# Sums of exponentials in four column tiles with a repeating load of the inverses, and convolutions in column halves beside layer 1

## The chip, the cores and the metric

The kernel runs on one core of a Trainium2 chip, in fp32 throughout. The metric is the device time of one execution in microseconds (us), from the median of several runs; lower is better. The engines of the core run side by side, each through its own queue in order: TensorE (PE, with its weight loads shown as PEld), VectorE (DVE), ScalarE (ACT), GpSimd (POOL), and SyncE (SP), which here only issues DMAs.

## The reference

The input x has 4 images of 128 channels and 64 x 64 positions, so S = 4096 positions per image. Two layers follow one another; the second ends with a mixture of experts.

```python
# layer 0: x + attention over positions, from 1x1 convolutions
xn    = group_norm(x)                       # 32 groups
e1    = prelu(w1 @ xn)                      # 64 channels (queries)
e2    = prelu(w2 @ xn)                      # 64 channels (keys)
asm   = prelu(wa @ xn)                      # 128 channels (values)
score = softmax(e1.T @ e2, axis=keys)       # 4096 x 4096 per image
x     = x + score @ asm.T
# layer 1: tokens t = x.T (4096 x 128)
t = t + softmax(q @ k.T / 128) @ v          # q, k, v from layer_norm(t)
t = t + expert_ffn(layer_norm(t))           # 64 experts, top 8 tokens of each
```

The softmax of layer 0 needs, for each query position, the sum of exponentials over all 4096 keys, and the product with the values is divided by it.

## The kernel before

**Tiling.** An image is cut into 8 blocks of 512 positions (`NB = 8`, `BLK = 512`). For a block of queries the keys are walked through in 8 steps (`NG = 8`) of 512 keys each. In a step, TensorE makes the scores of the current step (`ps`, L526), ScalarE takes their exponentials (`pt`, L535), and TensorE makes the products of the exponentials of the step before with the values (`av`, L460 in layer 0, L488 in layer 1). In layer 0 both matmul groups use TensorE as two row tiles (64 rows by 128 columns, printed as 64\*128). In layer 1 both use it as two column tiles (128\*64): the tuple `SCORE_COLS[1]` holds the two column halves. Everything that is fp32 goes through TensorE in two passes, so a matmul shows as two instructions.

**Stages and order.** `stage(b, layer, beside, then)` runs the attention of one image and layer as 64 steps. The order is written by hand: stages go (0,0), (1,0), (0,1), (2,0), (1,1), (3,0), (2,1), (3,1) as (image, layer). At each step, `step_after()` advances the finishing work of an earlier block by one segment, the query of the next block is prepared, and the generator `beside` advances by one segment. A `yield` in such a generator ends its segment. `tc.no_sync_barrier()` closes the step, so that instructions keep to their steps.

**Convolutions.** `conv(b)` computes e1, e2 and asm of an image, block by block, three segments each: normalise a block (`xn`); one matmul for e1 and e2 together (`pe`, L264, 128 by 128 weights, 512 columns moved); four matmuls for asm (`pa`, L280, 128 columns moved each). They run on the full array (128\*128). `conv(0)` and `conv(1)` run in the layer-0 stage (0,0); `conv(2)` runs beside the layer-1 stage (0,1) and `conv(3)` beside the layer-1 stage (1,1).

**Finishing a block of layer 0.** DVE adds the exponentials of all steps into `sacc` (L550), so that each of the 128 partitions holds the sum over its share of the keys. `finish_conv` then has three segments:

1. ScalarE copies the two halves of the product out of PSUM (`u`, `c0`), POOL adds them, DVE folds `sacc` to 128 x 512 (`c1`), POOL adds `c1` to a guard tile `all_sum`.
2. A matmul with a 128 x 128 matrix of ones (`pd`, L572) adds `c1` over the partitions and leaves each sum on all 128 partitions; DVE takes the reciprocal (`inv`, L574); POOL multiplies `u` by it (L575), adds it into a guard tile `all_inv` (L576) and adds the residual (`xp`, L578).
3. DVE transposes `xp` in 32 x 32 blocks (`xt`, L306) and SP stores it to DRAM for layer 1 (`xT`, L313).

`finish_conv` runs once per block: 32 times, 29 of them in steps of a layer-0 stage and 3 (block 7 of images 1, 2 and 3) in the first steps of a layer-1 stage. `finish_attn` does the same for layer 1, in eight segments; its matmuls `pv` (L614) and `pg` (L663), and the query matmul `pq` (L429), are in column halves already.

**Buffers.** `ms_tile` gives one of two PSUM banks to all small matmuls (`pd`, `pe`, `pa`, `pv`, `pg`, `pq`). `block_tile("inv", ...)` has two buffers in SBUF. POOL's queue carries `u`, `all_sum`, `all_inv`, `xp`, and the powers of -0.5 that layer norm needs (`l_y`, L174).

Of the kernel before, what the change touches and what calls it, by code (L numbers as in the profile page):

```python
# [15 lines left out]
P = 128  # L16
BLK = 512
# [5 lines left out]
SCORE_COLS = {0: (slice(0, P),), 1: (slice(0, P // 2), slice(P // 2, P))}  # L23
# [3 lines left out]
def tile_unshifted(  # L27
# [14 lines left out]
    nc = tc.nc  # L42
    x = a["x"]
    B, C, S = x.shape
# [4 lines left out]
    NB = S // BLK  # L49
    NJ = S // P  # L50
    SUB = BLK // P
# [24 lines left out]
    def ms_tile(name):  # L76
        return ps_ms.tile([P, BLK], F32, tag="ms", name=name)

    def block_tile(tag, name, bufs=2):
        pool = pools[of_pool.get(tag, "blk")]  # L80
        return pool.tile([P, BLK], F32, tag=tag, name=name, bufs=bufs)

    def dram_tile(shape, name):
        return dram.tile(shape, F32, tag=name, name=name)
# [6 lines left out]
    t2 = [[dram_tile([P, BLK], f"t2_{b}_{n}") for n in range(NB)] for b in range(B)]  # L91
    x1T = [[dram_tile([P, SUB, C], f"xT_{b}_{n}") for n in range(NB)] for b in range(B)]
    tokens = [dram_tile([S, C], f"tk_{b}") for b in range(B)]
    first_pair = dram_tile([P, S], "first_pair")

    e1 = [[dram_tile([CR, BLK], f"e1_{b}_{n}") for n in range(NB)] for b in range(B)]

    def load_block(tag, src, name, bufs):
        t = block_tile(tag, name, bufs)
        nc.sync.dma_start(out=t, in_=src)  # L100
        return t
# [6 lines left out]
    for i, q in enumerate((nc.sync, nc.scalar, nc.sync, nc.scalar)):  # L108
        part = bass.ts(i, S // 4)
# [8 lines left out]
    w12 = const_load("w12", [P, 2 * CR], a["w12T"])  # L118
    b12 = const_load("b12", [P, 1], a["b12"])
    a12 = const.tile([P, 1], F32, tag="a12", name="a12")  # L120
    for i, al in enumerate(("a1", "a2")):
        nc.scalar.dma_start(
            out=a12[i * CR : (i + 1) * CR, :], in_=a[al].partition_broadcast(CR)
        )
    wa = const_load("wa_sb", [P, C], a["waT"])
# [8 lines left out]
    for h in range(2):  # L134
# [6 lines left out]
    ones = const.tile([P, P], F32, tag="ones", name="ones")  # L141
# [8 lines left out]
        out=last, in_=last, compare_op=ALU.is_ge, fill=0.0, base=1 - P, pattern=[[0, P]],  # L150
# [9 lines left out]
        out=avg_g3, in_=avg_g3, compare_op=ALU.is_ge, fill=0.0, base=0,  # L160
# [3 lines left out]
        out=avg_g3, in_=avg_g3, compare_op=ALU.is_ge, fill=0.0, base=GS - 1,  # L164
# [18 lines left out]
    def group_norm(b, first=None):  # L183
        st = small.tile([P, NB, 6], F32, tag="gn_st", name=f"gn_st{b}")

        def pair(i):
            if i == NB // 2:
                return []
            if first is not None:
                return [first[:, bass.ts(2 * i + h, BLK)] for h in range(2)]  # L190
            return [
                load_block("xs", x_of(b, 2 * i + h), f"g{b}_{2 * i + h}", 4) for h in range(2)
            ]

        coming = pair(0)
        yield
        for i in range(NB // 2):
            blocks, coming = coming, pair(i + 1)
            for h in range(2):
                nc.vector.bn_stats(out=st[:, 2 * i + h, :], in_=blocks[h])  # L200
            yield
        mv = small.tile([P, 2], F32, tag="gn_mv", name=f"gn_mv{b}")
        nc.vector.bn_aggr(out=mv, in_=st.rearrange("p n s -> p (n s)"))
        yield
        pm = ms_tile(f"gn_pm{b}")
        nc.tensor.matmul(pm[:, 0:1], lhsT=avg_g, rhs=mv[:, 0:1], start=True, stop=True)
        ab = const.tile([P, 2], F32, tag=f"gn{b}", name=f"gn{b}")
        nc.vector.tensor_copy(ab[:, 0:1], pm[:, 0:1])
        d = small.tile([P, 2], F32, tag="gn_d", name=f"gn_d{b}")
        nc.vector.tensor_sub(d[:, 0:1], mv[:, 0:1], ab[:, 0:1])  # L210
        nc.vector.scalar_tensor_tensor(
            d[:, 1:2], in0=d[:, 0:1], scalar=d[:, 0:1], in1=mv[:, 1:2], op0=ALU.mult, op1=ALU.add
        )
        yield
        pv = ms_tile(f"gn_pv{b}")
        nc.tensor.matmul(pv[:, 0:1], lhsT=avg_g, rhs=d[:, 1:2], start=True, stop=True)
        inv_sqrt(ab[:, 1:2], pv[:, 0:1], GN_EPS, 1, f"gn{b}")
        gn[b] = ab
        yield
# [22 lines left out]
        for h in range(2):  # L242
            nc.sync.dma_start(out=q[h * CR : (h + 1) * CR, :], in_=src)

    def conv(b, whole=None):


        kA = seq.tile([P, NP, P], F32, tag="k", name=f"e2_{b}")
        vT = seq.tile([P, NJ, C], F32, tag="v", name=f"asm{b}")
        keys[b, 0], values[b, 0] = kA, vT  # L250

        def block(n):
            if whole is None:
                return load_block("xs", x_of(b, n), f"ck{b}_{n}", 4)
            return whole[:, bass.ts(n, BLK)]

        xb = block(0)
        for n in range(NB):
            xn = normed(b, xb, f"xk{b}_{n}")
            if n + 1 < NB:  # L260
                xb = block(n + 1)
            yield
            pe = ms_tile(f"pe{b}_{n}")
            nc.tensor.matmul(pe, lhsT=w12, rhs=xn, start=True, stop=True)  # L264
            y, t = block_tile("ye", f"ye{b}_{n}"), block_tile("te", f"te{b}_{n}")
            nc.scalar.activation(y, pe, AF.Identity, bias=b12)
            prelu([(y, lambda z: z)], y, t, a12)
            y4 = y[CR:, :].rearrange("c (p h t) -> c p h t", h=2, t=P)
            for h in range(2):
                nc.sync.dma_start(  # L270
                    out=kA[h * CR : (h + 1) * CR, bass.ts(n, SUB // 2), :], in_=y4[:, :, h, :]
                )
            if whole is not None and n == 0:
                spread_query(b, n, y[:CR, :])
            else:
                nc.sync.dma_start(out=e1[b][n], in_=y[:CR, :])
            yield
            pa = ms_tile(f"pa{b}_{n}")
            for s in range(SUB):
                nc.tensor.matmul(  # L280
                    pa[:, bass.ts(s, P)], lhsT=xn[:, bass.ts(s, P)], rhs=wa, start=True, stop=True
                )
            y2, t2 = block_tile("ye", f"ya{b}_{n}"), block_tile("te", f"ta{b}_{n}")
            y3 = y2.rearrange("p (s c) -> p s c", c=C)
            nc.vector.tensor_tensor(
                y3, pa.rearrange("p (s c) -> p s c", c=C),
                ba.unsqueeze(1).to_broadcast([P, SUB, C]), op=ALU.add,
            )
            prelu(
                [(vT[:, bass.ts(n, SUB), :], lambda z: z.rearrange("p (s c) -> p s c", c=C))],  # L290
                y2, t2, aa,
            )
            yield
# [9 lines left out]
    SQ = 32  # L303
# [256 lines left out]
    def finish_conv(b, n):  # L560
        nm = f"{b}_0_{n}"
        av = avs.pop((b, 0, n))
        u, c0, c1 = (block_tile(t, f"{t}{nm}") for t in ("u", "c0", "c1"))
        s2 = sums.pop((b, n))
        nc.scalar.copy(u, av[:, 0, :])
        nc.scalar.copy(c0, av[:, 1, :])
        nc.gpsimd.tensor_add(u, u, c0)
        nc.vector.tensor_add(c1, s2[:, 0, :], s2[:, 1, :])  # L568
        nc.gpsimd.tensor_add(all_sum, all_sum, c1)  # L569
        yield  # L570
        pd = ms_tile(f"pd{nm}")
        nc.tensor.matmul(pd, lhsT=ones, rhs=c1, start=True, stop=True)  # L572
        r = block_tile("inv", f"inv{nm}")
        nc.vector.reciprocal(r, pd)  # L574
        nc.gpsimd.tensor_mul(u, u, r)  # L575
        nc.gpsimd.tensor_add(all_inv, all_inv, r)  # L576
        xp = block_tile("xp", f"xp{nm}")
        nc.gpsimd.tensor_add(xp, resid.pop((b, 0, n)), u)  # L578
        yield
        turn_to_tokens(xp, block_tile("tb", f"xt{nm}"), x1T[b][n])  # L580
# [200 lines left out]
    def chain(*gens):  # L781
        for g in gens:
            yield from g
# [4 lines left out]
    def stage(b, layer, beside, then, ahead=None, pace=(6, 3)):  # L788

        coming = iter(())
        for k in range(pace[0]):
            next(ahead or iter(()), None)
        for n, g in attention(b, layer):
            step_after()
            if g == 1:
                coming = query(b, layer, n + 1) if n + 1 < NB else then and query(*then, 0)
                coming = coming or iter(())
            next(coming, None)  # L800
            if n == 0 and ahead:
                for _ in range(pace[1]):
                    next(ahead, None)
            else:
                next(beside, None)
            tc.no_sync_barrier()
        run(coming)
        run(beside)
# [38 lines left out]

    stage(0, 0, chain(group_norm(1), conv(1), weights_qk()), (1, 0), ahead=first_conv, pace=(3, 3))
    stage(1, 0, chain(group_norm(2), attn_keys(0), mix_values(0)), (0, 1))
    stage(0, 1, chain(group_norm(3), conv(2)), (2, 0))  # L850
    stage(2, 0, chain(done_after(route(0, take_from_seq(0))), attn_keys(1), mix_values(1)), (1, 1))
    stage(1, 1, conv(3), (3, 0))
    stage(3, 0, chain(done_after(route(1, take_from_seq(1))), attn_keys(2), mix_values(2)), (2, 1))
    stage(2, 1, attn_keys(3), (3, 1))
    ends["prep"].close()
# [118 lines left out]
    for i in range(B // 2):  # L974
        pe = ms_tile(f"poe{i}")
# [6 lines left out]
        for n in range(NB):  # L982
            px = sc_tile(f"px{i}_{n}")
            for h in range(2):
# [3 lines left out]
                    start=True, stop=True,  # L988
# [541 lines left out]
```

## Time and profile before

| | |
|---|---|
| median of 3 runs | 3368.74 us (3368.69 to 3370.04) |
| profiled execution | 3368.98 us |
| its span, first to last instruction | 3367.3 us |
| TensorE clock granted, mean | 0.986 |
| TensorE busy | 3261.8 us, 97% of the span |
| DVE, ACT, POOL busy | 2179.4, 1244.3, 432.2 us |
| `pd` matmuls (L572) | 64 instructions, 36.0 us |
| `pe` and `pa` matmuls (L264, L280) | 64 and 256 instructions, 37.6 and 38.2 us |
| reciprocal of layer 0 (L574) | 32 instructions, 3356 ns each |

Busy time counts a stretch once per group of instructions, so that groups whose instructions overlap add up to more than the engine's own busy time. Starts in the timeline are therefore a better measure of what a matmul costs than its listed duration: TensorE starts the next group before the last one has drained. The rows of the timeline are printed as start in us, length in us, engine, line, operation, output<-inputs, the tile of the array that is used, shape, and count of instructions in the row.

### The profile page before, as it was taken

Reading aid. Unit: us, or ns where it says so; the run is one execution under the profiler, and the core shown is the slowest. Engines: PE = TensorE matmul, PEld = TensorE weight load, DVE = VectorE, ACT = ScalarE, POOL = GpSimd, SP = SyncE. Lnnn points to the kernel's source line nnn. Section 1 sums busy time; section 2 is a strip of 40 time slices with the busy share of each in tenths; the row PEclk is TensorE's granted clock in tenths of the full one; section 3 lists DMA queues with packets and bytes.
Section 4 is the critical chain, followed back from the end, with each engine's and each line's share of the span. In section 5 each row is a group of like instructions: output and inputs, shape, how many; then the busy total and the mean of one; then the engine's idle time right before and its main releaser. Section 6 shows DMA issues by size and latency. Waiting matters only on the chain. (4 is left out here: it accounts for less than half of the span.)

```text
span 3367.3 us, 48432 instructions
## 1 busy us (share of the span) xinstructions
PE 3261.8 (97%) x19392; PEld 1539.9 (46%) x19392; DVE 2179.4 (65%) x4184; ACT 1244.3 (37%) x1417; POOL 432.2 (13%) x409
## 2 busy tenths in 40 slices
PE   7999999999999999999999999999999999999955
PEld 4444444444444444444445444444454545445432
DVE  6665577556675667756766567865775656765654
ACT  2333333333333344333333334333333333433320
POOL 0111122310000013230000003251000001100000
PEclk9999999999999999999999999999999999999977
DMA  3121122011110112201210111310321101120169
GB/s 86 44 47 24 37 55 62 19 32 40 40 41 23 36 26 51 62 16 29 47 36 19 30 33 54 69 39 18 66 47 27 26 23 32 32 70 16 26 239 348
DMA packets 359354, 174.13 MB, mean 52 GB/s; under 512 B 275280, under 2 KB 300752, under 8 KB 358864
## 3 DMA queue, kind: packets, MB, share of 16 engines
q1 hardware_dynamic: 351408, 159.71, 18.5%
q10 hardware_dynamic: 7200, 10.20, 0.8%
q8 instruction: 154, 2.52, 0.3%
q0 software_dynamic: 512, 1.05, 0.1%
q14 instruction: 80, 0.66, 0.1%
HBM read 110.20 MB, written 56.23 MB: 49 GB/s over the span
## 5 line engine op out<-in xcount | busy, mean ns | idle before, releaser
L535 ACT ACTIVATE pt<-ps 128x1024 f32<-128x1024 f32 x1024 | 1020.8, 1024 | 1566.3 <-PE ps L526 1475.3
L526 PE MATMUL ps<-q,t 128*64 128x512 f32 x4096 | 927.4, 594 | 0.0
L460 PE MATMUL av<-pt,asm 64*128 64x512 f32 x4096 | 922.1, 589 | 0.9 <-ACT sw L597 0.9
L550 DVE TENSOR_TENSOR sacc<-sacc,pt 128x1024 f32<-128x1024 f32 x448 | 570.5, 1273 | 203.3 <-ACT pt L535 171.9
L488 PE MATMUL av<-pt,tt 128*64 128x256 f32 x3072 | 638.0, 380 | 0.0
L460 PEld LDWEIGHTS av<-pt,asm 64*128 64x128 f32 x4096 | 396.1, 187 | 485.0 <-issue 470.5
L474 DVE TENSOR_TENSOR tt<-pt 128x512 f32<-128x512 f32 x512 | 353.4, 690 | 371.0 <-ACT pt L535 352.3
L488 PE MATMUL av<-tt,mixed 128*64 128x256 f32 x2048 | 527.4, 380 | 5.2 <-DVE tt L474 5.2
L526 PEld LDWEIGHTS ps<-q,t 128*64 128x64 f32 x4096 | 290.6, 137 | 497.8 <-issue 462.8
L526 PE MATMUL ps<-e,e 64*128 64x512 f32 x2048 | 490.5, 597 | 2.4 <-ACT pt L535 2.4
L488 PEld LDWEIGHTS av<-pt,tt 128*64 128x64 f32 x3072 | 354.1, 137 | 291.4 <-issue 143.2
L488 PE MATMUL av<-pt,mixed 128*64 128x256 f32 x1024 | 305.5, 380 | 0.0
L488 PE MATMUL av<-tt,tt 128*64 128x256 f32 x1024 | 305.5, 380 | 0.0
L526 PEld LDWEIGHTS ps<-e,e 64*128 64x128 f32 x2048 | 192.3, 187 | 245.9 <-issue 238.2
L488 PEld LDWEIGHTS av<-tt,mixed 128*64 128x64 f32 x2048 | 281.1, 137 | 8.8 <-DVE tt L474 6.1
L174 POOL TENSOR_TENSOR l_y<-l_v,mhalf 128x4 f32<-128x4 f32 x64 | 64.7, 1011 | 1691.3 <-DVE l_v L173 1691.3
L476 DVE TENSOR_TENSOR tt<-pt 128x256 f32<-128x256 f32 x512 | 221.8, 433 | 16.5
L475 DVE TENSOR_TENSOR pt<-tt,pt 128x256 f32<-128x256 f32 x512 | 218.6, 427 | 16.3
L488 PEld LDWEIGHTS av<-pt,mixed 128*64 128x64 f32 x1024 | 140.6, 137 | 73.1 <-DVE pt L475 0.3
L488 PEld LDWEIGHTS av<-tt,tt 128*64 128x64 f32 x1024 | 140.6, 137 | 2.0 <-issue 0.8
L574 DVE RECIPROCAL inv<-pd 128x512 f32<-128x512 f32 x32 | 107.4, 3356 | 29.4 <-PE pd L572 29.4
L569 POOL TENSOR_TENSOR all_sum<-all_sum,c 128x512 f32<-128x512 f32 x32 | 44.9, 1402 | 539.0 <-DVE c L568 539.0
(189 smaller groups left out, 1788.0 us busy)
## 6 DMA issues: line engine op xcount, KB each, us to landing
w<-in_weight_dram SPq DMA_DIRECT2D x32, 1024.0 KB, 14.2
xq<-in_x_dram SPq DMA_DIRECT2D x32, 256.0 KB, 4.2
xT<-xt SPq DMA_DIRECT2D x128, 64.0 KB, 2.2
ak<-xT SPq DMA_DIRECT2D x32, 256.0 KB, 3.1
t<-kt SPq DMA_DIRECT2D x128, 64.0 KB, 2.2
t<-t SPq DMA_DIRECT2D x32, 256.0 KB, 3.4
xr<-xT SPq DMA_DIRECT2D x32, 256.0 KB, 3.0
y<-x SPq DMA_DIRECT2D x32, 256.0 KB, 4.7
```

The costliest lines, as they stand in the source:

```text
L174: nc.gpsimd.tensor_tensor(y[:, :k], v[:, :k], mhalf[:, :k], op=ALU.pow)
L460: nc.tensor.matmul(avs[b, 0, n][:, r, :], lhsT=values[b, 0][rows, j, :], rhs=pt[rows, h, :], start=(j == 0), stop=(j == NJ - 1),)
L474: nc.vector.tensor_sub(tt[:, 0:2, :], p4[:, :, 1, :], p4[:, 0, :, :])
L475: nc.vector.tensor_add(p4[:, 0, 1, :], tt[:, 1, :], p4[:, 0, 0, :])
L476: nc.vector.tensor_sub(tt[:, 2, :], p4[:, 1, 0, :], p4[:, 0, 1, :])
L488: nc.tensor.matmul(av[bass.ts(half, HC), bank, slot, :], lhsT=lhsT, rhs=rhs, start=first, stop=final, skip_group_check=True,)
L526: nc.tensor.matmul(ps[part, h, :], lhsT=key[:, part], rhs=q[rows, :], start=True, stop=True,)
L535: nc.scalar.activation(pt, ps, AF.Exp, scale=scale)
L550: nc.vector.tensor_add(sums[b, n], sums[b, n], pt)
L569: nc.gpsimd.tensor_add(all_sum, all_sum, c1)
L574: nc.vector.reciprocal(r, pd)
```

## The change

The four edits:

- The matmul with ones becomes four, each with 32 columns of ones and 128 of the 512 query columns, on the four column tiles of 32 (128\*32). The sum of query column 128k + t lands on partitions 32k to 32k + 31 at column t, so the result is 128 x 128. The reciprocal and the guard addition work on 128 x 128.
- The inverses go to DRAM (one row of each group of 32 partitions, 4 x 128 values, 2 KB) and come back by a load that repeats the 512 values on all 128 partitions (`rb`, 256 KB written).
- `finish_conv` has five segments in place of three: the load and the multiplication stand one and two steps after the sums. What follows (`xp`, `xt`, `xT`) moves two steps later.
- `conv(2)` and `conv(3)` take `cols=SCORE_COLS[1]` and issue each matmul as two, one for each half of the columns.

```diff
+    inv0 = [[dram_tile([BLK], f"inv0_{b}_{n}") for n in range(NB)] for b in range(B)]
...
-    def conv(b, whole=None):
+    def conv(b, whole=None, cols=(slice(0, P),)):
...
-            nc.tensor.matmul(pe, lhsT=w12, rhs=xn, start=True, stop=True)
+            for part in cols:
+                nc.tensor.matmul(pe[part, :], lhsT=w12[:, part], rhs=xn, start=True, stop=True)
...
             for s in range(SUB):
-                nc.tensor.matmul(
-                    pa[:, bass.ts(s, P)], lhsT=xn[:, bass.ts(s, P)], rhs=wa, start=True, stop=True
-                )
+                for part in cols:
+                    nc.tensor.matmul(
+                        pa[part, bass.ts(s, P)], lhsT=xn[:, bass.ts(s, P)][:, part], rhs=wa,
+                        start=True, stop=True,
+                    )
...
-        pd = ms_tile(f"pd{nm}")
-        nc.tensor.matmul(pd, lhsT=ones, rhs=c1, start=True, stop=True)
-        r = block_tile("inv", f"inv{nm}")
+        pd = ms_tile(f"pd{nm}")[:, :P]
+        for k in range(SUB):
+            nc.tensor.matmul(
+                pd[bass.ts(k, SQ), :], lhsT=ones[:, :SQ], rhs=c1[:, bass.ts(k, P)],
+                start=True, stop=True,
+            )
+        r = block_tile("inv", f"inv{nm}")[:, :P]
         nc.vector.reciprocal(r, pd)
-        nc.gpsimd.tensor_mul(u, u, r)
-        nc.gpsimd.tensor_add(all_inv, all_inv, r)
+        nc.gpsimd.tensor_add(all_inv[:, :P], all_inv[:, :P], r)
+        nc.sync.dma_start(
+            out=inv0[b][n].rearrange("(k t) -> k t", k=SUB),
+            in_=r.rearrange("(k i) t -> k i t", i=SQ)[:, 0, :],
+        )
+        yield
+        rb = block_tile("inv", f"rb{nm}")
+        nc.sync.dma_start(out=rb, in_=inv0[b][n].partition_broadcast(P))
+        yield
+        nc.gpsimd.tensor_mul(u, u, rb)
         xp = block_tile("xp", f"xp{nm}")
         nc.gpsimd.tensor_add(xp, resid.pop((b, 0, n)), u)
         yield
...
-    stage(0, 1, chain(group_norm(3), conv(2)), (2, 0))
+    stage(0, 1, chain(group_norm(3), conv(2, cols=SCORE_COLS[1])), (2, 0))
...
-    stage(1, 1, conv(3), (3, 0))
+    stage(1, 1, conv(3, cols=SCORE_COLS[1]), (3, 0))
```

## Prediction

> **What bounds the kernel now.** I read the page's busy line, then TensorE's timeline (start, length, row), then waits and DMAs.
>
> ```profile
> PE 3261.8 (97%) x19392; PEld 1539.9 (46%) x19392; DVE 2179.4 (65%) x4184; ACT 1244.3 (37%) x1417; POOL 432.2 (13%) x409
> ```
>
> TensorE never rests in the attention stages. What a small matmul costs is read from starts, in a layer-0 stage first:
>
> ```profile
> 84.96 3.60 PE L460 MATMUL av<-pt,asm 64*128 64x512 f32 x16
> 88.49 1.13 PE L572 MATMUL pd<-c,ones 128*128 128x512 f32 x2
> 89.55 1.99 PE L526 MATMUL ps<-e,e 64*128 64x512 f32 x8
> 91.37 3.60 PE L460 MATMUL av<-pt,asm 64*128 64x512 f32 x16
> 94.80 1.88 PE L526 MATMUL ps<-e,e 64*128 64x512 f32 x8
> 96.52 3.60 PE L460 MATMUL av<-pt,asm 64*128 64x512 f32 x16
> 99.95 1.88 PE L526 MATMUL ps<-e,e 64*128 64x512 f32 x8
> ```
>
> A plain step, scores to scores, is 99.95 − 94.80 = 5.15 us (the median of 188 such steps). From av to av across `pd` it is 91.37 − 84.96 = 6.41: about 1.2 us more, with no idle time printed. By scores to scores, steps with `pd` take 6.30, so `pd` costs 1.15. Then a layer-1 stage (rows of L488 left out):
>
> ```profile
> 878.72 1.12 PE L264 MATMUL pe<-xk,w 128*128 128x512 f32 x2
> 879.77 3.65 PE L526 MATMUL ps<-q,t 128*64 128x512 f32 x16
> ...
> 886.28 1.03 PE L429 MATMUL pq<-t,wqk 128*64 128x512 f32 x4
> 887.24 1.16 PE L280 MATMUL pa<-wa_sb,xk 128*128 128x128 f32 x8
> 888.33 3.65 PE L526 MATMUL ps<-q,t 128*64 128x512 f32 x16
> ...
> 894.83 3.60 PE L526 MATMUL ps<-q,t 128*64 128x512 f32 x16
> ...
> 901.39 1.12 PE L264 MATMUL pe<-xk,w 128*128 128x512 f32 x2
> 902.44 3.65 PE L526 MATMUL ps<-q,t 128*64 128x512 f32 x16
> ```
>
> Here a plain step is 6.46 (median of 134), one with `pe` 7.61 (894.83 to 902.44), with `pa` 7.69, with `pd` 7.66, and with `pq`, in column halves, 7.32. So the full-array groups cost 1.15, 1.23 and 1.20, and the halves 0.86. All four stream as many columns: 512, twice over, at the same rate; the surplus is what the full array adds among halves.
>
> Four narrow tiles appear only in the expert part:
>
> ```profile
> 3265.90 1.08 PE L939 MATMUL po<-w,hT 128*32 128x128 f32 x32
> 3266.80 0.61 PE L909 MATMUL ph<-w,pooledT 128*32 128x512 f32 x3
> ```
>
> 32 instructions of 128 columns, four sets of 8, take 0.90 us: 0.225 per set, with its weights. One such set is what the new `pd` issues. Last, the other engines:
>
> ```profile
> L574 DVE RECIPROCAL inv<-pd 128x512 f32<-128x512 f32 x32 | 107.4, 3356 | 29.4 <-PE pd L572 29.4
> DVE xt L306 <- POOL xp L578: 105.1, 30, 3.9
> xT<-xt SPq DMA_DIRECT2D x128, 64.0 KB, 2.2
> t<-t SPq DMA_DIRECT2D x32, 256.0 KB, 3.4
> ```
>
> Per block DVE spends 3.36 us in the reciprocal and then 3.5 waiting for `xp`, yet TensorE's plain steps stay at 5.15. DVE is not the bound; a small DMA lands in 2.2 us, a block load in 3.4.
>
> **What the Trainium skill says.** "TensorEngine Tiling (Array Packing)", Key Properties: changing the tiling mode drains TensorE, whereas different tiles of one mode load weights and multiply in parallel. The trace agrees: `pq` costs 0.86 between other halves, and 1.11 between row tiles (6.26 − 5.15); four narrow weight loads and matmuls fit in 0.225 us. "DMA: Bandwidth & Descriptors", Anatomy of one DMA, gives a DMA (fitted on GpSimd's path) about 2 us that no size reduces, mostly the receipt of the write; the 2.2 us of the 64 KB stores is of that size, so I price the 2 KB store by it.
>
> **The change, part by part.**
>
> *pd.* The stream falls to a quarter, 0.225 us. To it comes the change of mode in and out. Column halves among row tiles show it: `pq` 1.11 − 0.86 = 0.25 (0.86 being its cost where the mode stays), and `pg`, half the columns, 0.68 − 0.43 = 0.25 (its step takes 5.83). I take 0.25: 0.475 in all. No row shows narrow tiles between row tiles. Below, 0.40: part of the 0.25 is the first weight load, and that of 32 columns is shorter (115 against 137 ns). Above, 0.77: the full-array `pwv`, also 128 columns, costs 0.61 (5.76 − 5.15), 0.40 more than its stream, plus three further loads of about 0.05. Saved: 29 in layer-0 stages at 1.15 − 0.475 = 0.675, 19.6 us; 3 in layer-1 stages at 1.20 − 0.475 = 0.725, 2.2. In four steps `pd` stands with `pe`, `pa`, `pwqk` or `pe` (7.16, 7.30, 6.63, 8.52), where now one change of mode served both; neighbours then differ in mode, 0.2 lost each. **21.0 us** (12 to 23.5).
>
> *Convolutions.* 16 `pe` of 1.15 and 16 `pa` of 1.23 become halves. `pe` then has the shape of `pq`, `pa` that of `pv` (128\*64, 129 columns; step 7.33, so 0.87): 16 x 0.29 + 16 x 0.37 = 4.6 + 5.9, **10.5 us** (8 to 11.5). Three of these steps also have TensorE waiting about 2 us for `xT` by DVE (the two PSUM banks of `ms_tile` are both taken by `pv`); nothing here shortens that.
>
> *DVE.* The reciprocal of 128 columns lies between 512 columns (3356 ns) and 3 (170): 0.170 + 125 x 6.26 ns = 0.95 us. 32 x 2.4 = 77 us go from DVE, and probably most of the 105 us waiting for `xp`, as `xt` now stands behind two more steps of additions. I cost this at **nothing** for the end: TensorE hides it, and no plain step waits for DVE. If TensorE stopped being the bound it would be a gain.
>
> *POOL.* `all_inv` falls from 1300 ns to about a quarter, 32 x 0.9 us, off the path. The multiplication (1268 ns) and `xp` stay.
>
> *SP and the new waits.* 32 stores of 2 KB and 32 loads (8.4 MB written, 5% of the traffic), each some 0.4 us of SP issue (`xq` took 0.42). The store waits for the reciprocal, the load for the store; behind them on SP are `g`, `ck` and `ak` loads and e1/e2 stores. These loads come a segment or more before use, and the next query is asked for at its second step, seven ahead; a hold of 2.2 us reaches nobody. Cost **nothing**, upper bound in the rival below. On POOL the multiplication waits for `rb`; behind it stand `xp`, and `l_y` in the stages with `attn_keys`, for which DVE waits. The chain from `pd`'s start: 0.5 + 0.95 + 2.2 + 3.4 + 1.27 + 1.27 = 9.6 us to `xp`. `xt` now comes after the additions of two further steps: before, it ran at 96.91, 8.4 us after `pd`; now it may run from about 98.5. So `xp` is on time or under 1 us late. The `xT` stores come two steps, 10 us, later; nothing reads them within a stage's first steps except block 0, long stored. Both tiles of the pair `inv` are now used per block, but the last reader is done four steps before the next `pd`.
>
> *Sum.* 21.0 + 10.5 = 31.5 us. Against the profiled execution (3367.3 span, 3368.98 whole): 3337.5. The median is 0.24 lower: **3337.2**.
>
> **The rivals.**
>
> 1. *Narrow tiles bring nothing between row tiles* (15%). If drain and eight weight loads and matmuls ran in sequence, `pd` would stay at about 1.15: four matmuls of 2 x 128 columns one after another are as long as one of 512. Only the convolutions gain: 3368.74 − 10.5 = 3358.2. Against: 0.225 us per set in the expert part; for: that row has no change of mode within it.
> 2. *The halves bring nothing* (6%): 3368.7 − 21.0 = 3347.7. For: twice the weight loads. Against: `pq` and `pv` among the same neighbours. It is also the case in which an edit does not do what it says.
> 3. *Both fail* (3%): no change, 3366 to 3369.
> 4. *Slower: the repeating load is late* (3%). Place: POOL's multiplication, then `xp`, then DVE at `xt`, with the additions to `sacc` behind it; these free `pt`, on which ScalarE's exponentials and so TensorE's scores depend. DVE has carried 3.36 + 3.5 us per block without a stall and now carries 0.95, so 5.9 us are spare. From there each microsecond costs up to 32 us in all. To pass +0.2% it must eat 31.5 + 6.7 us, 1.2 per block: `rb` has to land 7 us later than worked out, store and load together in some 12.7 instead of 5.6; then 3376 or more. For: SP's queue is in order, and `rb` can stand behind e1/e2 stores that wait for DVE. Against: 128 rows of 2 KB are a plain block load, and DMA's busy share in these stages is mostly 1 to 2 tenths.
>
> **How the numbers follow.** The likeliest case, with 73%, is that both parts pay: 3337.2, itself 3333 to 3348 by the bounds of `pd` and the convolutions. Rivals 1 and 2 lie just above. The range of 3332 to 3352 takes in the likeliest case and rival 2, and leaves out rival 1 except for partial forms of it, and 3 and 4. Faster by over 0.2% (6.7 us, about what a measurement of this kernel can tell from no change): 73 + 15 + 6 = 94%. Within: 3%. Slower: 3%.
>
> **What would show it.** Right: TensorE's starts give about 5.63 for layer-0 steps with `pd`, 7.32 for layer-1 steps with `pe` or `pa`, and 5.15 and 6.46 still for plain ones; `xt`'s wait for `xp` mostly gone; L574's successor near 0.95 us. Wrong: steps with `pd` above 5.92 (narrow tiles dear), layer-1 steps above 7.5 (halves dear), or plain steps of the layer-0 stages longer than 5.15 with idle time put down to ScalarE or DVE (`rb` late).

## The result, and the profile after

The changed kernel takes 3349.0 us (median of 4 runs, 3346.99 to 3351.32) against 3368.95 before: a ratio of 0.994, 95% interval 0.9923 to 0.9958. It is faster by about 20 us, inside the range and short of the 31.5 us forecast. The profiled execution took 3348.11 us, 20.9 less than the one before.

The page of the kernel after, its busy line first:

```profile
PE 3234.1 (97%) x19744; PEld 1585.2 (47%) x19744; DVE 2122.9 (63%) x4184; ACT 1244.3 (37%) x1417; POOL 401.7 (12%) x409
```

TensorE has shed 27.7 us of busy time, but the span only 20.9: some idle time is new. The same stretches of TensorE's timeline as before (start, length, row), a layer-0 stage:

```profile
84.85 3.60 PE L465 MATMUL av<-pt,asm 64*128 64x512 f32 x16
88.38 0.42 PE L579 MATMUL pd<-c,ones 128*32 128x128 f32 x8
88.73 1.99 PE L531 MATMUL ps<-e,e 64*128 64x512 f32 x8
90.56 3.60 PE L465 MATMUL av<-pt,asm 64*128 64x512 f32 x16
93.99 1.88 PE L531 MATMUL ps<-e,e 64*128 64x512 f32 x8
```

and a layer-1 stage (rows of L493 left out):

```profile
865.90 1.06 PE L267 MATMUL pe<-xk,w 128*64 128x512 f32 x4
866.76 3.63 PE L531 MATMUL ps<-q,t 128*64 128x512 f32 x16
...
873.22 1.06 PE L434 MATMUL pq<-t,wqk 128*64 128x512 f32 x4
874.07 1.07 PE L284 MATMUL pa<-wa_sb,xk 128*64 128x128 f32 x16
874.95 3.63 PE L531 MATMUL ps<-q,t 128*64 128x512 f32 x16
...
881.40 3.63 PE L531 MATMUL ps<-q,t 128*64 128x512 f32 x16
```

From av to av across `pd` it is now 90.56 − 84.85 = 5.71 us where it was 6.41. By scores to scores a step with `pd` takes 5.60 in place of 6.30, one with `pe` 7.31 in place of 7.61, one with `pa` 7.33 in place of 7.69. Plain steps are still 5.15 and 6.46. So the matmuls gained what was forecast. What is missing shows in one place of TensorE's timeline, in stage (2,0), and again in stage (3,0):

```profile
1256.18 3.60 PE L465 MATMUL av<-pt,asm 64*128 64x512 f32 x16
1263.86 0.69 PE L766 MATMUL pool<-twin,halves 128*128 128x64 f32 x2 [4.09 <-DVE halves L760]
1264.48 3.28 PE L531 MATMUL ps<-e,e 64*128 64x512 f32 x8
```

`pool` is the small product by which the router (`route`, run beside the attention) pools the tokens that it has gathered (`got`): DVE makes their weights (`r_wgt`) and their weighted sum (`halves`), which TensorE takes as it stands. TensorE waits 4.09 us for DVE's `halves` (4.77 in stage (3,0)); in the kernel before these steps had no such wait. Why `halves` is late is read from DVE and POOL in the same stretch. DVE after:

```profile
1250.71 0.71 DVE L311 STREAM_TRANSPOSE xt<-xp 128x512 f32<-128x512 f32 x1 [4.74 <-POOL xp L596]
1251.35 2.51 DVE L555 TENSOR_TENSOR sacc<-sacc,pt 128x1024 f32<-128x1024 f32 x2
...
1254.21 4.19 DVE L749 TENSOR_SCALAR r_wgt<-r_w,inv_tot 64x4 f32<-64x4 f32 x2
1258.44 0.28 DVE L758 TENSOR_SCALAR halves<-got,r_wgt 128x128 f32<-128x128 f32 x1
1258.76 5.05 DVE L760 SCALAR_TENSOR_TENSOR halves<-got,r_wgt,halves 128x128 f32<-128x128 f32 x3
```

POOL after:

```profile
1241.75 2.01 POOL L731 DMA_INDIRECT got<-tk,r_rows  x1 [5.48 <-DVE r_rows L729]
...
1247.09 0.94 POOL L731 DMA_INDIRECT got<-tk,r_rows  x1 [0.31 <-issue]
1248.05 1.28 POOL L594 TENSOR_TENSOR u<-u,rb 128x512 f32<-128x512 f32 x1
1249.41 1.27 POOL L596 TENSOR_TENSOR xp<-xq,u 128x512 f32<-128x512 f32 x1
1253.42 4.95 POOL L771 TENSOR_TENSOR M<-M,z 64x1024 f32<-64x1024 f32 x2 [2.75 <-ACT z L770]
1258.57 4.70 POOL L771 TENSOR_TENSOR M<-M,z 64x1024 f32<-64x1024 f32 x2 [0.20 <-ACT z L770]
```

The router's four gathers now stand on POOL ahead of the moved multiplication `u*rb`; `xp` comes at 1250.7; DVE waits 4.74 us for it at the transpose; and the router's small operations on DVE then run while POOL subtracts `M − z` (which leaves the exponentials of the chosen tokens). In the kernel before, DVE was just past them when POOL began, by 0.5 us here and by 0.3 us in stage (3,0). DVE before, and POOL's subtraction:

```profile
1268.57 0.46 DVE L731 TENSOR_SCALAR r_wgt<-r_w,inv_tot 64x4 f32<-64x4 f32 x2
1269.07 0.29 DVE L740 TENSOR_SCALAR halves<-got,r_wgt 128x128 f32<-128x128 f32 x1
1269.39 1.12 DVE L742 SCALAR_TENSOR_TENSOR halves<-got,r_wgt,halves 128x128 f32<-128x128 f32 x3
1270.43 11.10 DVE L550 TENSOR_TENSOR sacc<-sacc,pt 128x1024 f32<-128x1024 f32 x4
```

```profile
1271.03 12.70 POOL L753 TENSOR_TENSOR M<-M,z 64x1024 f32<-64x1024 f32 x4 [5.88 <-ACT z L752]
```

Two `r_wgt` of 4 columns take 4.19 us in place of 0.46, three `halves` 5.05 in place of 1.12. The slowing itself is not new: before, it fell on the four additions to `sacc` that came next, 11.10 us in place of 5.2, and TensorE did not wait for those. So the profile before already showed both the slowing and how close `halves` stood to it.

The wait has a second price, in the clock granted to TensorE. The columns are the stretch, its length, the busy time of PE, PEld, DVE, ACT and POOL (with counts), the clock, the share of DMA and its GB/s:

```profile
1260.00:1264.00 4.00, 0.14 (x1) 0.14 (x1) 3.93 (x4) 0.00 (x0) 3.36 (x3) 0.96 0.00 0
1264.00:1268.00 4.00, 4.00 (x12) 1.93 (x14) 3.69 (x4) 1.21 (x2) 0.00 (x0) 0.61 0.00 0
```

After 4 us without work the clock falls to 0.61 for the next 4, and the scores take 3.28 us in place of 1.88.

### The profile page after: what moved, and what is told of

Read it like the earlier page. It is cut to its first block, busy times and chain, and to the rows that moved or that the text cites. A ratio compares the mean times of both kernels' runs of the same rounds, so it can differ in the third digit from the quotient of the medians.

```text
span 3346.4 us, 49254 instructions
## 1 busy us (share of the span) xinstructions
PE 3234.1 (97%) x19744; PEld 1585.2 (47%) x19744; DVE 2122.9 (63%) x4184; ACT 1244.3 (37%) x1417; POOL 401.7 (12%) x409
## 5 line engine op out<-in xcount | busy, mean ns | idle before, releaser
L540 ACT ACTIVATE pt<-ps 128x1024 f32<-128x1024 f32 x1024 | 1021.0, 1024 | 1552.0 <-PE ps L531 1477.9
L555 DVE TENSOR_TENSOR sacc<-sacc,pt 128x1024 f32<-128x1024 f32 x448 | 577.7, 1289 | 306.7 <-ACT pt L540 281.5
L493 PE MATMUL av<-pt,tt 128*64 128x256 f32 x3072 | 638.0, 380 | 0.0
L531 PEld LDWEIGHTS ps<-q,t 128*64 128x64 f32 x4096 | 308.9, 137 | 476.1 <-issue 447.5
L493 PE MATMUL av<-tt,mixed 128*64 128x256 f32 x2048 | 527.6, 380 | 5.2 <-DVE tt L479 5.2
L493 PEld LDWEIGHTS av<-pt,tt 128*64 128x64 f32 x3072 | 358.2, 137 | 271.0 <-issue 139.9
L493 PE MATMUL av<-tt,tt 128*64 128x256 f32 x1024 | 305.7, 380 | 0.0
L493 PE MATMUL av<-pt,mixed 128*64 128x256 f32 x1024 | 305.5, 380 | 0.0
L493 PEld LDWEIGHTS av<-tt,mixed 128*64 128x64 f32 x2048 | 281.4, 137 | 8.8 <-DVE tt L479 6.1
L493 PEld LDWEIGHTS av<-pt,mixed 128*64 128x64 f32 x1024 | 140.6, 137 | 64.9 <-DVE pt L480 0.3
L493 PEld LDWEIGHTS av<-tt,tt 128*64 128x64 f32 x1024 | 140.7, 138 | 2.0 <-issue 0.8
L552 DVE TENSOR_TENSOR sacc<-pt,pt 128x1024 f32<-128x1024 f32 x32 | 42.3, 1323 | 55.9 <-ACT pt L540 55.9
```

The costliest lines, as they stand in the source:

```text
L493: nc.tensor.matmul(av[bass.ts(half, HC), bank, slot, :], lhsT=lhsT, rhs=rhs, start=first, stop=final, skip_group_check=True,)
L531: nc.tensor.matmul(ps[part, h, :], lhsT=key[:, part], rhs=q[rows, :], start=True, stop=True,)
L540: nc.scalar.activation(pt, ps, AF.Exp, scale=scale)
L552: nc.vector.tensor_add(sums[b, n], pts[0], pts[1])
L555: nc.vector.tensor_add(sums[b, n], sums[b, n], pt)
```

## The experiments

**The convolutions alone.** The kernel before, with the change's `cols` in `conv` and

```diff
-    stage(0, 1, chain(group_norm(3), conv(2)), (2, 0))
+    stage(0, 1, chain(group_norm(3), conv(2, cols=SCORE_COLS[1])), (2, 0))
-    stage(1, 1, conv(3), (3, 0))
+    stage(1, 1, conv(3, cols=SCORE_COLS[1]), (3, 0))
```

> The kernel before with the column halves in conv(2) and conv(3) alone. Theory (the terms add up, and the 11 us missing from the forecast were lost in two stalls of the routing steps, which the convolutions do not touch): 16 x (1.15 - 0.86) + 16 x (1.23 - 0.86) = 10.5 us less, 3358.4; layer-1 steps with pe or pa at 7.32, all others as before, no wait of TensorE for DVE's halves beyond the 24 us of the last image. Rival (the halves lose elsewhere what they save in their steps): 3364 or more.

Measured: 3356.36 us, ratio 0.9966 (0.9952 to 0.9979). `pe` steps 7.31, `pa` steps 7.33 (one of them, just after a wait for `xT`, 9.02). From the start of the first of these stages to the end of the second, TensorE's timeline gains 9.8 us against before (739.56 to 1992.32 there, 738.39 to 1981.31 here); the rest lies at the kernel's two ends. No new wait for `halves`. The halves are worth what their steps say.

**The sums alone.** The changed kernel, with the convolutions put back.

```diff
-    stage(0, 1, chain(group_norm(3), conv(2, cols=SCORE_COLS[1])), (2, 0))
+    stage(0, 1, chain(group_norm(3), conv(2)), (2, 0))
-    stage(1, 1, conv(3, cols=SCORE_COLS[1]), (3, 0))
+    stage(1, 1, conv(3), (3, 0))
```

> The changed kernel with the full-array convolutions put back, so the four narrow tiles, the repeating load and the longer finish alone. Theory: 29 x 0.70 + 3 x 0.70 = 22.4 us less on the matmuls, of which about 10.6 are given back in the steps of image 2 and 3 in which TensorE takes the routing's small product: 3357.5, with two waits of TensorE for DVE's halves of 4 to 5 us. Rival (the missing 11 us come from the two parts together, or from drift): 3347, no such waits.

Measured: 3358.39 us, ratio 0.9973 (0.9963 to 0.9982), with both waits in full, 4.11 and 4.76 us. So the loss belongs to the sums' part, not to the two together.

**The transpose two steps later.** The changed kernel, with

```diff
         nc.gpsimd.tensor_add(xp, resid.pop((b, 0, n)), u)
         yield
+        yield
+        yield
         turn_to_tokens(xp, block_tile("tb", f"xt{nm}"), x1T[b][n])
```

> The changed kernel with the transpose of xp two steps later (two more segments in finish_conv), so that DVE no longer waits for xp ahead of the routing's small operations. Theory (POOL's multiplication stands behind four gathers, DVE waits 4.7 us at the transpose, and its weights and halves then fall into POOL's subtraction M-z, which slows them): DVE has its halves some 5 us earlier, before or as POOL begins to subtract; no stall, all of the forecast: 3337.5. Rival (POOL's subtraction, which starts 1.9 us earlier since the reciprocal is shorter, meets the halves in any case): half of the stalls or more stays, 3342 to 3348.

Measured: 3341.88 us, ratio 0.9921 (0.9907 to 0.9935): about half came back, close to the rival's 3342 to 3348. But the rival's reason does not hold: POOL's subtraction begins 1.03 us ahead of the step's scores in the kernel before and 1.04 in the changed kernel and in this one (stage (2,0)), so the shorter reciprocal did not bring it forward. TensorE still waits 1.34 us in stage (2,0) and 4.23 in stage (3,0). DVE in stage (3,0) of this kernel, and POOL beside it:

```profile
2035.24 4.87 DVE L555 TENSOR_TENSOR sacc<-sacc,pt 128x1024 f32<-128x1024 f32 x2 [1.79 <-ACT pt L540]
...
2040.60 4.64 DVE L751 TENSOR_SCALAR r_wgt<-r_w,inv_tot 64x4 f32<-64x4 f32 x2
...
2045.59 5.26 DVE L762 SCALAR_TENSOR_TENSOR halves<-got,r_wgt,halves 128x128 f32<-128x128 f32 x3
```

```profile
2035.54 1.27 POOL L594 TENSOR_TENSOR u<-u,rb 128x512 f32<-128x512 f32 x1
2036.89 2.14 POOL L596 TENSOR_TENSOR xp<-xq,u 128x512 f32<-128x512 f32 x1
2040.54 4.67 POOL L773 TENSOR_TENSOR M<-M,z 64x1024 f32<-64x1024 f32 x2 [1.51 <-ACT z L772]
```

DVE no longer waits for `xp`, but its two additions, 2.5 us alone, take 4.87 beside POOL's `u*rb` and `xp`, and so it is late again. The first of the two additions, 2.66 us long, is over before ScalarE's exponentials of z begin at 2039.26, so these are not what slows it. My theory had only the wait at the transpose; the late work on POOL delays DVE by running beside it just as well.

**The subtraction one step later.** The changed kernel, with one more segment in `route` of images 0 and 1 ahead of the exponentials of z and the subtraction:

```diff
         nc.vector.tensor_copy(pooled[:, :, b], pq[:, :E])
+        if b < 2:
+            yield
         subtract = nc.vector.tensor_sub if b == B - 1 else nc.gpsimd.tensor_sub
```

> The changed kernel with the exponentials of z and POOL's subtraction M-z of images 0 and 1 one step later than the routing's small product; DVE's wait of 4.7 us at the transpose stays. Theory (the slowing by POOL's subtraction is what makes the halves late): r_wgt and halves take 1.9 us in place of 9.5 and are ready 3 us before TensorE asks for them; no stall: 3337.5. Rival (the 4.7 us wait alone makes them late): the stalls stay at 4 us or more each, 3348.

Measured: 3332.89 us, ratio 0.9897 (0.9882 to 0.9912). DVE still waits 4.75 us for `xp`, and yet:

```profile
1250.79 0.71 DVE L311 STREAM_TRANSPOSE xt<-xp 128x512 f32<-128x512 f32 x1 [4.75 <-POOL xp L596]
...
1254.30 0.46 DVE L749 TENSOR_SCALAR r_wgt<-r_w,inv_tot 64x4 f32<-64x4 f32 x2
1254.79 0.29 DVE L758 TENSOR_SCALAR halves<-got,r_wgt 128x128 f32<-128x128 f32 x1
1255.12 1.13 DVE L760 SCALAR_TENSOR_TENSOR halves<-got,r_wgt,halves 128x128 f32<-128x128 f32 x3
```

The same operations at the same time, with POOL idle: 1.9 us in place of 9.6, and `pool` starts at its place without a wait. The stalls need POOL's subtraction. (ScalarE's exponentials of z moved along with it; the slow addition in the run above was slow without them.) Between the profiled executions this run gains 16.7 us on the changed kernel. Of these, 13.5 are the four steps at the two stalls; 1.6 in stage (1,1) and 1.1 in stage (3,1) lie in steps that the edit does not touch. The 3337.5 expected held neither these nor the gain of DVE that is named below.

**The routing three steps later.** The changed kernel, with the number of idle steps ahead of the router as an argument of `done_after`, 9 by default as before:

```diff
-chain(done_after(route(0, take_from_seq(0))), attn_keys(1), mix_values(1))
+chain(done_after(route(0, take_from_seq(0)), NG + 4), attn_keys(1), mix_values(1))
-chain(done_after(route(1, take_from_seq(1))), attn_keys(2), mix_values(2))
+chain(done_after(route(1, take_from_seq(1)), NG + 4), attn_keys(2), mix_values(2))
```

> The changed kernel with the routing of images 0 and 1 started three steps later within their stages, its inner order untouched, so that its gathers stand on POOL behind the multiplication by rb and not ahead of it. Theory A (what makes the halves late is the meeting of the routing with the longer finish of a block: gathers ahead of u*rb and xp on POOL): no wait of TensorE for halves, as with the later subtraction: 3333. Theory B (the routing alone brings its halves and POOL's subtraction together, once the reciprocal no longer holds DVE): stalls of 1 to 4 us stay: 3340 to 3348.

Measured: 3333.57 us, ratio 0.9896 (0.9881 to 0.9911), no wait for `halves`. The inner order of the routing is unchanged, only its place against the finish of a block: `u*rb` runs at 1240.89 and the gathers at 1259.76. It bears out theory A, but does not test the gathers alone: POOL's subtraction now also stands behind the next block's additions and starts at 1274.55, after DVE has made `halves` (by 1271.9).

**The shorter reciprocal alone.** The kernel before, with

```diff
-        nc.vector.reciprocal(r, pd)
-        nc.gpsimd.tensor_mul(u, u, r)
-        nc.gpsimd.tensor_add(all_inv, all_inv, r)
+        r = r[:, :P]
+        nc.vector.reciprocal(r, pd[:, :P])
+        r4 = r.unsqueeze(1).to_broadcast([P, SUB, P])
+        u3 = u.rearrange("p (s c) -> p s c", c=P)
+        a3 = all_inv.rearrange("p (s c) -> p s c", c=P)
+        nc.gpsimd.tensor_tensor(u3, u3, r4, op=ALU.mult)
+        nc.gpsimd.tensor_tensor(a3, a3, r4, op=ALU.add)
```

> The kernel before with one thing changed: the reciprocal of layer 0 takes only the first 128 of 512 columns (0.95 in place of 3.36 us) and POOL uses these four times over; the other inverses are left out. Theory A: DVE is 2.4 us earlier throughout, the two long steps ahead of each routing product (6.14 and 5.30 in place of 5.15) become plain, no new stall: about 2.8 us less, 3365.5. Theory B: z and so POOL's subtraction come 2.4 us earlier and meet the halves: TensorE waits for halves in images 2 and 3, up to 10 us more, 3375.

The kernel leaves out the inverses of the other 384 columns; only its time is of use. Measured: 3363.28 us, ratio 0.9983 (0.9976 to 0.9990), no wait for `halves`. TensorE's rows of stage (2,0), before and then in this kernel:

```profile
1255.47 1.88 PE L526 MATMUL ps<-e,e 64*128 64x512 f32 x8
1257.19 3.60 PE L460 MATMUL av<-pt,asm 64*128 64x512 f32 x16
1261.61 2.04 PE L526 MATMUL ps<-e,e 64*128 64x512 f32 x8 [0.82 <-ACT pt L535]
```

```profile
1256.37 1.88 PE L526 MATMUL ps<-e,e 64*128 64x512 f32 x8
1258.09 3.60 PE L460 MATMUL av<-pt,asm 64*128 64x512 f32 x16
1261.52 1.88 PE L526 MATMUL ps<-e,e 64*128 64x512 f32 x8
```

A step of 6.14 us becomes 5.15. So DVE was the bound before in these few steps, where the reciprocal stood between two scans of 4.4 us for the router; a shorter one is worth 1.1 us in stage (2,0) and 1.9 in (3,0). Theory B falls. The remaining 1.7 us between the two profiled executions lie at the start and in the last stage; their cause is open.

**The sums in two column halves.** The kernel with the later subtraction, and (with the reciprocal, `all_inv` and the store widened to 256 columns alike)

```diff
-        pd = ms_tile(f"pd{nm}")[:, :P]
-        for k in range(SUB):
+        pd = ms_tile(f"pd{nm}")[:, :HB]
+        for k in range(2):
             nc.tensor.matmul(
-                pd[bass.ts(k, SQ), :], lhsT=ones[:, :SQ], rhs=c1[:, bass.ts(k, P)],
+                pd[bass.ts(k, HC), :], lhsT=ones[:, :HC], rhs=c1[:, bass.ts(k, HB)],
```

> The kernel with the later subtraction, and the sums in two column halves of 256 columns in place of four narrow tiles of 128. Theory (the stream shrinks with the columns moved, the change of mode stays at about 0.25): pd costs 0.43 + 0.25 = 0.68 in place of 0.45, layer-0 steps with pd 5.83; 32 x 0.23 = 7.4 us more than with narrow tiles, 3340. Rival (most of the saving is the smaller weight load and not the stream): 5.65 or less, 3335.

Measured: 3343.63 us, ratio 0.9922 (0.9906 to 0.9937). Steps with `pd` take 5.83: 0.68 us, as worked out. The whole is 3.6 us longer than the 3340 expected; in the profiled execution one plain step of stage (1,1) takes 8.15 us in place of 6.46, and one in stage (3,0) 5.75 in place of 5.18; the rest is open. With 512, 256 and 128 columns to stream, the cost is 1.15, 0.68 and 0.45: halving the stream takes 0.47 and then 0.23. By this line, an estimated 0.22 us do not depend on the stream.

**Halves in all convolutions.** The kernel with the later subtraction, and

```diff
-    first_conv = conv(0, first_x)
+    first_conv = conv(0, first_x, SCORE_COLS[1])
...
-    stage(0, 0, chain(group_norm(1), conv(1), weights_qk()), (1, 0), ahead=first_conv, pace=(3, 3))
+    stage(0, 0, chain(group_norm(1), conv(1, cols=SCORE_COLS[1]), weights_qk()), (1, 0), ahead=first_conv, pace=(3, 3))
```

> The kernel with the later subtraction, and column halves in conv(0) and conv(1) too, beside the row tiles of layer 0. Theory (a group of halves among row tiles costs 0.86 + 0.25 = 1.11, as pq does): pe 1.15 to 1.11, pa 1.28 to 1.11, pe with pa 2.15 to 1.97: 8 x 0.21 + 6 x 0.18 = 2.8 us less, 3330. Rival (the gain of halves is only that the mode does not change): no difference, 3333.

Measured: 3331.61 us, ratio 0.9887 (0.9872 to 0.9903). `pe` among row tiles costs 1.11 as expected, but `pa` 1.22, where 1.11 was expected and the full array takes 1.29; both in one step 2.08 in place of 2.15. That is 8 x (0.04 + 0.07) + 6 x 0.07 = 1.3 us, as much as the two medians differ, though the single times overlap: only the steps tell theory and rival apart, and they bear out `pe` and not `pa`. Why `pa` keeps 0.11 more is open. It is the lowest median of all kernels here, 17 us under the changed kernel.

## Why the prediction was right, and where it was not

- **pd: right.** 0.475 was forecast, 0.45 measured. Twenty-eight steps gain 0.70; the three shared ones in layer 0 0.5 each, as forecast, and the shared one in layer 1 about 0.36 for its `pd`: 21.5 us against 21.0. Four narrow tiles between row tiles do run side by side, which no row of the trace before could show; rival 1 is out.
- **Convolutions: right.** 9.8 us against 10.5. The three groups in steps with `pv` gained little or nothing, since TensorE waits there for `xT` by DVE either way. Rival 2 is out.
- **DVE at nothing: wrong, by 2.8 us of gain.** I read the median of plain steps and took it for all. Two steps in each of two stages were held by DVE, 6.14 and 5.30 beside the router's scans, 6.88 and 5.31 in the other stage. In the changed kernel all but the last of them are plain.
- **POOL and the new waits at nothing: wrong, and the step that failed.** I listed what stands behind the moved multiplication on POOL (`xp`, `l_y`), and not what the move puts ahead of it: the router's gathers, which before came after `xp`. My list of what POOL's queue carries left out both the gathers and the subtraction `M − z`. The price of the two stalls, with the slowed steps that follow: 10.02 − 5.61 and 6.55 − 5.25 in stage (2,0), 5.7 us; 10.70 − 5.61 and 7.94 − 5.25 in stage (3,0), 7.8. Together 13.5.
- **Sum.** 21.5 + 9.8 + 2.8 − 13.5 = 20.6, against 20.9 measured between the profiled executions. That the result lies inside the range is in part luck: the range was made wide for matmuls that gain less, and these gained what was forecast. It took in a loss that it was not made for, with 3 us to spare at its upper end, since a gain of 2.8 that was also put at nothing made up for part of it.
- **Rival 4** named the right place, POOL's multiplication, `xp` and DVE's transpose, but the wrong cause and the wrong way out. The load was not late: `rb` was issued at 1237.38 and lands in 3.4 us (median), which is 7 us before the multiplication. And the wait reached TensorE not through `sacc`, `pt` and the exponentials but through a matmul that takes DVE's output directly, for which DVE's spare 5.9 us did not count. In blocks without routing DVE's wait at `xt` nearly vanished: 105.1 us in all before, now 14.1, of which 9.5 are the two waits beside the router:

```profile
DVE xt L311 <- POOL xp L596: 14.1, 6, 4.7
```

Why DVE is slow beside POOL is not shown by a run that takes the ports apart. "SBUF — State Buffer", Who interferes with whom, in the Trainium skill, says that a DVE instruction with two SBUF inputs and a GpSimd instruction that reads SBUF block one another for a whole instruction. The trace agrees for `halves` (two tensors): the first two of the three take 2.32 and 2.31 us, and each ends 0.15 us after one of the two subtractions of POOL from 1258.57 on (2.35 and 2.38 us); the third, which follows them, takes 0.35. The two `r_wgt`, of 4 columns, likewise take 1.87 and 2.30 us and end with the two subtractions before (within 0.03 us), which speaks for waiting a whole instruction rather than for a shared rate. But `r_wgt` reads one tensor and one number per partition, which is not the case named above; why it waits too was not tested.

## What to carry to other kernels

When a step is moved on an engine in order, look at what it is moved past in the stages where a second generator uses that engine too, and at every matmul that reads the slow side's result directly: those have none of the slack that a buffered chain has. A full-array matmul among tiles of another shape pays for the change of mode, and the gain of the right shape can be read from its neighbours: to a few hundredths of a microsecond for `pd`, and for `pe` and `pa` beside layer 1, less well (0.11) for `pa` beside layer 0. An operation that ends a few tenths of a microsecond before another engine begins is a warning, even where nothing waits yet. The median of plain steps hides the few that something else bounds; list the outliers before an engine is costed at nothing.

## What the runs showed of the hardware that I had not expected

DVE and POOL do not slow one another in proportion: two DVE operations of 4 columns took 4.19 us in place of 0.46 beside POOL's subtractions, and two additions of 1024 columns 4.87 in place of 2.5 beside two POOL operations. And a wait of 4 us cost TensorE more than itself, as the clock was granted at 0.61 (0.50 in stage (3,0)) for about 4 us afterwards: the scores then took 3.28 and 3.79 us in place of 1.88. The wait of 1.34 us, with the transpose two steps later, had no such sequel: the step after it took 5.26 us, as it does without a wait.
